# Fetching label rows of an embedding table one by one from SyncE in place of gathers on GpSimd

## The chip, the cores and the metric

The kernel runs on one core of a Trainium2 chip. A core has five engines that run their own instruction streams [...]: TensorE (matmuls, the transposes here too), VectorE (DVE), ScalarE (ACT), GpSimd (POOL) and SyncE (SP), which computes nothing and issues transfers. The metric is the device time of the whole program in microseconds, the median of the timed runs. A profile is a separate execution, recorded by the hardware profiler.

## The reference

The computation is the forward pass of a recommendation model on 16,384 samples. Each sample has 69 feature ids and one label id, all of them rows of an embedding table of 100,001 rows x 96 floats.

```python
u = emb[batch_user]                          # 16384 x 69 x 96
ql = emb[batch_label[:, 0]]                  # 16384 x 96
q = broadcast(ql[:, None, :], u.shape)
z = concatenate([q, u, q - u, q * u], -1)    # 384 wide
h = dice(z @ W1 + b1, a1)                    # 64 wide
att = (h @ W2 + b2) @ W3 + b3                # one number per feature
pre = where(batch_user < 100000, u * att, 0)
pooled = einsum('gf,bfe->bge', window, pre)  # 69 features into 10 groups
x = concatenate([pooled, ql], -1)            # 11 x 96 wide
h = dice(bn(x @ Wf1 + bf1), af1)             # 200 wide
h = dice(bn(h @ Wf2 + bf2), af2)             # 80 wide
return h @ Wf3 + bf3
```

dice(x, a) is (a (1 - p) + p) x with p = sigmoid(x). All values are float32. What matters here: 16,384 x 69 = 1,130,496 feature rows and 16,384 label rows of 384 bytes each are fetched by index from the table in HBM.

## The kernel before, in words

The samples are cut into 32 blocks of 512. The 512 x 69 feature rows of a block are cut into 69 chunks of 512 rows: 64 main chunks (8 samples x 64 features) and 5 tail chunks (512 samples x one feature). Two chunks make a pair, the unit of the main loop: 1,104 pairs in all, 34.5 to a block.

Gathers. `gather` (L226-232) is one indirect transfer issued by GpSimd: it fetches 128 table rows, whose numbers stand in a column of an SBUF tile, one to each of 128 partitions. A pair needs eight of them (`fetch`, L307). TensorE transposes what came (L308), VectorE multiplies it by the label's embedding (L311 or L318), ScalarE copies it (L319).

Label rows. A block's 512 label rows are fetched by four more gathers into a tile `q` (`head_gather`, L238-243), 128 rows each. `head_turn` (L245-249) transposes them on TensorE and puts the result into one of two tiles `qTs`; `head_row` (L251-269) multiplies that by the part of W1 that depends on the label alone. Tile `q` has two buffers.

Indices. `load_ids` (L100-103) has SyncE load one block's indices: 276 columns of feature ids and four of label ids. `map_ids` (L105-109) on VectorE moves the id 100,000 to a row of zeros. Its result, `rows`, is what the feature gathers read.

The rest of a pair's work. `seed` (L275-296) puts the label's share of the hidden layer into PSUM, `hidden` (L322-331) adds the two matmul terms of each chunk (L326) and applies dice (L328-330), `attend_rows` and `spread` (L333-365) turn four pairs of hidden values into attention weights, `pool` (L367-393) contracts them with the gathered rows (L376). When a block is through, its top network runs in ten steps (`top_steps`, L438-449); the last one, `top3`, stores 512 results by a transfer from SyncE (L432).

The order of work is written out by hand. Inside the manual schedule (L470) instructions go to their engines' queues in program order. In step i of the loop (L474-507) stand the seed of pair i-1, the pooling of pair i-8, the attention of pairs i-3 and i-4, the hidden layer of pair i-2 and the fetch of pair i, and after them what a plan (L452-468) has for that step. For block n with first pair `first`, the plan has the load of indices 24 steps ahead, `map_ids` 21, `head_gather` 14, `head_turn` 11 and `head_row` 9 steps ahead. The top network of a block begins 12 steps after its last pair, so the store of its result comes 21 steps after it. The gathered tiles `u` have 14 buffers, and a pair's tile is held until it is pooled 8 steps later.

The semaphores that count a transfer's completion are given out by the framework, which reuses a set of them in turn.

Of the kernel before, what the change touches and what calls it, by code (L numbers as in the profile page):

```python
# [30 lines left out]
F32 = mybir.dt.float32  # L31
# [6 lines left out]
P = 128  # L38
B, F, E, G = 16384, 69, 96, 10
ITEM_NUM = 100000  # L40
# [4 lines left out]
BLK = 512  # L45
NBLK = B // BLK
# [5 lines left out]
NQ = BLK // P  # L52
NT = NCH * 4
NCOL = NT + NQ
NPAIR = NBLK * NCH // 2
S_DICE = float(1.0 / np.sqrt(1.0 + 1e-9))
S_BN = float(1.0 / np.sqrt(1.0 + 1e-5))
# [6 lines left out]
def rec_kernel(  # L64
    ctx: ExitStack,
    tc: tile.TileContext,
    idx: bass.AP,
    emb: bass.AP,
    W1: bass.AP,
    b1: bass.AP,  # L70
# [17 lines left out]
    nc = tc.nc  # L88
# [8 lines left out]
    bpool = ctx.enter_context(tc.tile_pool(name="bpool", bufs=2))  # L97
    xpool = ctx.enter_context(tc.tile_pool(name="xpool", bufs=1))

    def load_ids(n):  # L100
        ids = ipool.tile([P, NCOL], I32, tag="ids", name=f"ids{n}")
        nc.sync.dma_start(out=ids, in_=idx[n : n + 1].rearrange("o p n -> (o p) n"))
        return ids

    def map_ids(n, ids):  # L105

        rows = ipool.tile([P, NT], I32, tag="rows", name=f"rows{n}")
        nc.vector.scalar_tensor_tensor(rows, ids[:, 0:NT], float(ITEM_NUM), ids[:, 0:NT], ALU.is_ge, ALU.add)
        return rows

    ids, rows = {0: load_ids(0)}, {}
# [9 lines left out]
    for i in range(2):  # L121
        nc.vector.tensor_add(Cq[0:E, i, :], w1[:, 0, :], w1[:, 2, :])
    nc.sync.dma_start(
        out=Cq[E : E + 1], in_=b1.rearrange("(o q h) -> o q h", o=1, q=1).to_broadcast([1, 2, H1])
# [101 lines left out]
    def gather(dst, index):  # L226
        nc.gpsimd.indirect_dma_start(  # L227
            out=dst,
            out_offset=None,
            in_=emb,  # L230
            in_offset=bass.IndirectOffsetOnAxis(ap=index, axis=0),
        )

    def chunk(c):

        return divmod(c, NCH)

    def head_gather(n):  # L238

        q = bpool.tile([P, NQ, E], F32, tag="q", name=f"q{n}")  # L240
        for k in range(NQ):
            gather(q[:, k, :], ids[n][:, NT + k : NT + k + 1])
        return q

    def head_turn(n, q):  # L245
        pq = ps_x.tile([E, BLK], F32, tag="x", name=f"pq{n}")
        for k in range(NQ):
            nc.tensor.transpose(pq[:, k * P : (k + 1) * P], q[:, k, :], ident)
        nc.vector.tensor_copy(qTs[n % 2][0:E, 0:BLK], pq)

    def head_row(n):  # L251

        cT = bpool.tile([P, BLK], F32, tag="cT", name=f"cT{n}")
        pc = ps_x.tile([P, BLK], F32, tag="x", name=f"pc{n}")
        for i in range(2):
            nc.tensor.matmul(
                pc[i * H1 : (i + 1) * H1, :],
                Cq[:, i, :],
                qTs[n % 2][:, i * NS : i * NS + BLK],
                start=True,  # L260
                stop=True,
            )
        nc.scalar.copy(cT, pc)

        cU = bpool.tile([P, BLK], F32, tag="cU", name=f"cU{n}")
        pc = ps_x.tile([P, BLK], F32, tag="x", name=f"pc2_{n}")
        nc.tensor.matmul(pc, Cq.rearrange("e i h -> e (i h)"), qTs[n % 2][:, 0:BLK], start=True, stop=True)
        nc.scalar.copy(cU, pc)
        return cT, cU
# [5 lines left out]
    def seed(i):  # L275

        ph = ps_h.tile([P, 512], F32, tag="h", name=f"ph{i}")
        nc.tensor.matmul(ph, zrow[:, 0:P], zrow, start=True, stop=False)  # L278
        (n0, k0), (n1, k1) = chunk(2 * i), chunk(2 * i + 1)
        if n0 == n1 and k1 < NMAIN:  # L280
            nc.scalar.copy(  # L281
                ph.rearrange("h (s f) -> h s f", f=FM), by_field(cs[n0][0][:, k0 * NS : (k0 + 1) * NS])
            )
        elif n0 == n1 and k0 >= NMAIN:
            nc.scalar.copy(ph, cs[n0][1])
        else:
            for j, (n, k) in enumerate([(n0, k0), (n1, k1)]):
                lo, hi = j * H1, (j + 1) * H1
                if k < NMAIN:
                    nc.scalar.copy(  # L290
                        ph[lo:hi].rearrange("h (s f) -> h s f", f=FM),
                        by_field(cs[n][1][lo:hi, k * NS : (k + 1) * NS]),
                    )
                else:
                    nc.scalar.copy(ph[lo:hi], cs[n][1][lo:hi, :])
        return ph
# [36 lines left out]
    def attend_rows(b, ys):  # L333

        pr = ps_x.tile([P, 512], F32, tag="x", name=f"prow{b}")
        for k, y in enumerate(ys):
            nc.tensor.matmul(pr[32 * k : 32 * (k + 1), :], v2, y, start=True, stop=True)  # L337
        row = rpool.tile([P, 512], F32, tag="row", name=f"row{b}")
        nc.scalar.copy(row, pr)  # L339
        return row  # L340

    def attend_tail(i, j, y, uT):

        n, k = chunk(2 * i + j)
        pa = ps_x.tile([E, 512], F32, tag="x", name=f"pa{i}_{j}")
        nc.tensor.matmul(pa, vrep[j * H1 : (j + 1) * H1, :], y[j * H1 : (j + 1) * H1, :], start=True, stop=True)  # L346
        nc.vector.scalar_tensor_tensor(pres[n][:, k - NMAIN, :], pa, bb[0:E], uT[:, j, :], ALU.add, ALU.mult)  # L347
# [88 lines left out]
    cs, pooled, pres, x1s, x2s, qs, us, hs, phs, ys, bands, rws, p1s = ({} for _ in range(13))  # L436

    def top_steps(n):  # L438


        def half(h, part):
            if h == 0 and part == 0:
                x1s[n] = xpool.tile([DH, 2, BLK], F32, tag="x1", name=f"x1_{n}")
            p1s[n] = top1(n, h, part, p1s.get(n))

        steps = [lambda h=h, part=part: half(h, part) for h in range(2) for part in range(4)]
        steps.append(lambda: x2s.__setitem__(n, top2(n)))
        steps.append(lambda: top3(n, x2s.pop(n)))
        return steps
# [4 lines left out]
    def at(step, work):  # L454
        plan.setdefault(step, []).append(work)

    for n in range(NBLK):
        first, end = n * NCH // 2, ((n + 1) * NCH - 1) // 2
        if n > 0:
            at(first - 24, lambda n=n: ids.__setitem__(n, load_ids(n)))  # L460
            at(first - 21, lambda n=n: rows.__setitem__(n, map_ids(n, ids[n])))
            at(first - 14, lambda n=n: qs.__setitem__(n, head_gather(n)))
            at(first - 11, lambda n=n: head_turn(n, qs.pop(n)))
            at(first - 9, lambda n=n: cs.__setitem__(n, head_row(n)))
        for s, work in enumerate(top_steps(n)):
            at(end + POOL_LAG + 4 + s, work)
    for f in range(NTAIL):
        at(2 + 2 * f, lambda f=f: tail_weights(f))

    with tc.manual_schedule():  # L470
        qs[0] = head_gather(0)
        head_turn(0, qs.pop(0))
        cs[0] = head_row(0)
        for i in range(NPAIR + POOL_LAG + 16):  # L474
            if 0 <= i - 1 < NPAIR:
                phs[i - 1] = seed(i - 1)
            if 0 <= i - POOL_LAG < NPAIR:
                k = i - POOL_LAG
                pool(k, us.pop(k), rws[k // 4])
                if k % 4 == 3:  # L480
                    rws.pop(k // 4)
            if 0 <= i - 3 < NPAIR and (i - 3) % 4 == 3:
                b = (i - 3) // 4
                bands[b] = attend_rows(b, [ys[4 * b + k] for k in range(4)])
            if 0 <= i - 3 < NPAIR:
                k = i - 3
                uT = hs.pop(k)[0]
                for j in range(2):
                    if chunk(2 * k + j)[1] >= NMAIN:
                        attend_tail(k, j, ys[k], uT)  # L490
            if 0 <= i - 4 < NPAIR and (i - 4) % 4 == 3:
                b = (i - 4) // 4
                rws[b] = spread(b, bands.pop(b))
                for k in range(4):
                    ys.pop(4 * b + k)
            if 0 <= i - 2 < NPAIR:
                ys[i - 2] = hidden(i - 2, phs.pop(i - 2), *hs[i - 2])
            if i < NPAIR:
                for j in range(2):
                    n, k = chunk(2 * i + j)  # L500
                    if n not in pooled:
                        pooled[n] = bpool.tile([E, G, BLK], F32, tag="pooled", name=f"pooled{n}")
                        pres[n] = xpool.tile([E, NTAIL, BLK], F32, tag="pre", name=f"pre{n}")
                u, uT, quT = fetch(i)
                us[i], hs[i] = u, (uT, quT)
            for work in plan.pop(i, []):
                work()
# [48 lines left out]
```

## Time and profile before

The time is 11,344.07 us, the median of 3 runs (11,340.12 to 11,345.51).

| | profiled execution |
|---|---|
| span | 13,499.4 us |
| granted TensorE clock, mean | 0.658 |
| TensorE busy | 10,109.4 us, 75% |
| GpSimd busy | 8,525.6 us, 63% |
| ScalarE busy | 3,740.6 us, 28% |
| VectorE busy | 3,172.4 us, 24% |
| gathers of feature rows | 8,832, mean 951 ns |
| gathers of label rows | 128, mean 963 ns |
| share of the 16 DMA engines taken by gathers | 15.5% |
| transfers issued by SyncE in the loop | 2 per block |

How to read it: the profile lists an instruction of each engine with its start, its duration, and the idle time ahead of it, and names what ended that idle time. "issue" means that nothing was seen to be waited for. "remote" is a releaser that the profile could not name among this core's instructions. "SPq" and "POOLq" are the instruction streams of SyncE and GpSimd where they issue transfers or wait; this is not counted as busy. [...] Note that the profiled execution is 19% longer than the timed ones.

### The profile page before, as it was taken

The page shows a single profiled execution, that of the slowest core. Times are in us where ns is not written, and L with a number is a line of the kernel's source. Part 1 is how long each engine was busy: PE and PEld are TensorE (multiplying, and loading weights), DVE is VectorE, ACT ScalarE, POOL GpSimd, SP SyncE. Part 2 cuts the span into 40 slices and gives each one's busy share as a digit, 9 for nine tenths or more (in the row PEclk, how much of TensorE's full clock was granted, in tenths as well). Part 3 has the DMA queues.
Part 4 walks back from the last instruction along what each step waited for, and adds up shares of the span by engine and source line. Part 5 has one row for each costly group of instructions (what it writes and reads, how often), then busy time and mean ns, then how long its engine had stood idle before and what let it go on. Part 6 is the DMA issues. An engine that isn't in the chain of part 4 may idle for free.

```text
span 13499.4 us, 108113 instructions
## 1 busy us (share of the span) xinstructions
PE 10109.4 (75%) x41348; PEld 5068.4 (38%) x41348; DVE 3172.4 (24%) x5424; ACT 3740.6 (28%) x6086; POOL 8525.6 (63%) x8966
## 2 busy tenths in 40 slices
PE   4777777778777776777777777777778777787778
PEld 2333333334333333333333333333333333343334
DVE  2222222222222222222222222222222222222222
ACT  1222222223222222222222222222222222232222
POOL 6666666666666666666666666666666666666664
PEclk5666666666666677666666666766666666666657
DMA  1111111111111111111111111111111111111111
GB/s 37 34 34 35 33 34 33 34 35 34 34 34 34 34 34 33 33 34 34 33 34 34 34 34 35 34 33 33 33 35 34 34 33 34 35 34 33 34 32 22
DMA packets 295008, 453.59 MB, mean 34 GB/s; under 512 B 145952, under 2 KB 151104, under 8 KB 294496
## 3 DMA queue, kind: packets, MB, share of 16 engines
q0 software_dynamic: 286720, 440.98, 15.5%
q8 instruction: 331, 5.42, 0.2%
q1 hardware_dynamic: 6142, 4.77, 0.1%
q14 instruction: 181, 1.48, 0.0%
q10 hardware_dynamic: 1634, 0.94, 0.0%
HBM read 446.04 MB, written 0.07 MB: 33 GB/s over the span
## 4 chain that ended last, share of the span: by engine, by line
PE 62%; another core or an unknown queue 15%; issue 12%; ACT 5%; DVE 5%; POOL 1%; DMA 0%; DVEq 0%; POOLq 0%; ACTq 0%
PE ph L326 22%; PE acc L376 15%; PE ptr L308 9%; PE p L406 5%; PE prow L337 4%; PE ph L278 4%; DVE y L330 3%; ACT y L329 2%; PE patt L353 2%; ACT y L328 1%; PE pa L346 1%; DVE quT L311 1%; ACT uT L319 1%; POOL u L227 1%
## 5 line engine op out<-in xcount | busy, mean ns | idle before, releaser
L227 POOL DMA_INDIRECT u<-in_emb,rows x8832 | 8401.6, 951 | 4802.4 <-issue 2351.7
L376 PEld LDWEIGHTS acc<-rw,u 128*96 128x96 f32 x16384 | 2185.5, 230 | 2828.8 <-issue 2828.2
L278 PE MATMUL ph<-zrow 1*128 1x512 bf16 x1104 | 532.2, 482 | 2654.8 <-DVE y L330 1760.5
L319 ACT COPY uT<-ptr 96x512 f32<-96x512 f32 x2208 | 1285.2, 582 | 3713.4 <-DVE quT L311 2616.7
L376 PE MATMUL acc<-rw,u 128*96 128x20 f32 x16384 | 2298.9, 292 | 1.8 <-DVE rw L359 1.3
L308 PEld LDWEIGHTS ptr<-ident,u 128*96 128x96 f32 x8832 | 1312.6, 167 | 1912.8 <-issue 1547.8
L308 PE MATMUL ptr<-ident,u 128*96 128x128 f32 x8832 | 1785.7, 362 | 326.1 <-issue 247.9
L326 PE MATMUL ph<-uT,A 96*64 96x512 f32 x4416 | 1954.0, 955 | 27.4 <-issue 26.7
L326 PE MATMUL ph<-quT,w 96*64 96x512 f32 x4416 | 1915.7, 909 | 54.5 <-issue 53.2
L328 ACT ACTIVATE y<-ph 128x512 f32<-128x512 f32 x1104 | 659.4, 597 | 4602.9 <-remote 2107.1
L330 DVE TENSOR_TENSOR y<-ph,y 128x512 f32<-128x512 f32 x1104 | 763.7, 692 | 4689.6 <-ACT y L329 2396.5
L311 DVE TENSOR_TENSOR quT<-ptr,qT 96x512 f32<-96x512 f32 x2048 | 1340.0, 680 | 1866.9 <-remote 887.1
L385 DVE COPY pooled<-acc 96x160 f32<-96x160 f32 x1008 | 430.6, 427 | 2811.6 <-remote 1020.7
L326 PEld LDWEIGHTS ph<-quT,w 96*64 96x64 f32 x4416 | 491.4, 202 | 1279.1 <-issue 1277.6
L329 ACT ACTIVATE y<-y,a1c,na1c 128x512 f32<-128x512 f32 x1104 | 897.4, 813 | 37.2
L281 ACT COPY ph<-cT 128x512 f32<-128x512 f32 x1008 | 591.4, 587 | 281.5 <-remote 75.0
L406 PE MATMUL p<-pooled,wf 96*100 96x512 f32 x1280 | 620.0, 625 | 6.3 <-issue 4.8
L337 PE MATMUL prow<-y,v 128*32 128x512 f32 x2208 | 546.6, 932 | 79.7 <-issue 41.3
L326 PEld LDWEIGHTS ph<-uT,A 96*64 96x64 f32 x4416 | 307.0, 183 | 766.4 <-issue 696.0
L339 ACT COPY row<-prow 128x512 f32<-128x512 f32 x276 | 161.4, 585 | 864.0 <-remote 345.4
L353 PE MATMUL patt<-ident,row 128*128 128x128 f32 x1104 | 267.9, 386 | 113.4 <-DVE pre L347 88.1
L406 PEld LDWEIGHTS p<-pooled,wf 96*100 96x100 f32 x1280 | 219.7, 181 | 270.1 <-issue 267.3
(71 smaller groups left out, 2535.6 us busy)
## 6 DMA issues: line engine op xcount, KB each, us to landing
u<-in_emb,rows POOLq DMA_INDIRECT x8832
ids<-in_idx SPq DMA_DIRECT2D x32, 140.0 KB
q<-in_emb,ids POOLq DMA_INDIRECT x128
wf<-in_Wf ACTq DMA_DIRECT2D x1, 825.0 KB
out<-res SPq DMA_DIRECT2D x32, 2.0 KB
w<-in_W SPq DMA_DIRECT2D x1, 96.0 KB
wf<-in_Wf ACTq DMA_DIRECT2D x1, 62.5 KB
a1c<-in_a SPq DMA_DIRECT2D x2, 0.2 KB
```

The costliest lines, as they stand in the source:

```text
L227: nc.gpsimd.indirect_dma_start(out=dst, out_offset=None, in_=emb, in_offset=bass.IndirectOffsetOnAxis(ap=index, axis=0),)
L278: nc.tensor.matmul(ph, zrow[:, 0:P], zrow, start=True, stop=False)
L308: nc.tensor.transpose(ptr[:, t * P : (t + 1) * P], u[:, 4 * j + t, :], ident)
L311: nc.vector.tensor_tensor(quT[:, j, :].rearrange("e (s f) -> e s f", f=FM), ptr.rearrange("e (s f) -> e s f", f=FM), by_field(q[:, k * NS ...
L319: nc.scalar.copy(uT[:, j, :], ptr)
L326: nc.tensor.matmul(ph[j * H1 : (j + 1) * H1, :], w, x[:, j, :], start=False, stop=last)
L328: nc.scalar.activation(y, ph, AF.Sigmoid, scale=S_DICE)
L329: nc.scalar.activation(y, y, AF.Identity, bias=a1c, scale=na1c)
L330: nc.vector.tensor_mul(y, ph, y)
L337: nc.tensor.matmul(pr[32 * k : 32 * (k + 1), :], v2, y, start=True, stop=True)
L376: nc.tensor.matmul(pa[:, j, 2 * t : 2 * t + 2, :].rearrange("e n g -> e (n g)"), u[:, 4 * j + t, :], rw[:, i % 4, j, t, :], start=True, st ...
L406: nc.tensor.matmul(p1, w[:, h * DH : (h + 1) * DH], x, start=(k == 0), stop=(k == KTOP - 1))
```

## The change

Blocks 1 to 31 no longer gather their label rows on GpSimd. Instead SyncE loads 32 labels at a time into its registers from a new input `lab` (the labels in plain order), and issues one transfer per label, from the table row that the register names to one partition of `q`. A block takes 16 such parts; part k stands in the plan 31 - k steps ahead of the block, from 31 to 16 steps. Block 0 keeps its four gathers (`first_head`). Tile `q`, what reads it, and everything else stay as they were. The purpose is to take work from GpSimd and give it to SyncE.

```diff
+NLD = 32
...
+    lab: bass.AP,
...
-    def head_gather(n):
-
-        q = bpool.tile([P, NQ, E], F32, tag="q", name=f"q{n}")
+    def first_head():
+
+        q = bpool.tile([P, NQ, E], F32, tag="q", name="q0")
         for k in range(NQ):
-            gather(q[:, k, :], ids[n][:, NT + k : NT + k + 1])
+            gather(q[:, k, :], ids[0][:, NT + k : NT + k + 1])
         return q
+
+    def head_gather(n, part):
+
+        if part == 0:
+            qs[n] = bpool.tile([P, NQ, E], F32, tag="q", name=f"q{n}")
+        k, p = divmod(part * NLD, P)
+        _, at = nc.values_load_multi_w_load_instructions(
+            lab[n : n + 1, part * NLD : (part + 1) * NLD],
+            engines=[mybir.EngineType.SP],
+            min_val=0,
+            max_val=ITEM_NUM,
+            skip_runtime_bounds_check_because="labels are rows of the table",
+        )
+        for i, row in enumerate(at):
+            nc.sync.dma_start(out=qs[n][p + i : p + i + 1, k, :], in_=emb[bass.ds(row, 1), :])
...
-            at(first - 14, lambda n=n: qs.__setitem__(n, head_gather(n)))
+            for part in range(BLK // NLD):
+                at(first - 31 + part, lambda n=n, part=part: head_gather(n, part))
             at(first - 11, lambda n=n: head_turn(n, qs.pop(n)))
...
-        qs[0] = head_gather(0)
-        head_turn(0, qs.pop(0))
+        head_turn(0, first_head())
...
+        "lab": x["batch_label"].reshape(NBLK, BLK),
```

More of the change, by code (lines that the diff above doesn't have):

```diff
@@ L518 @@
     tail = user[:, :, FM:].reshape(NBLK, NQ, P, NTAIL).transpose(0, 2, 3, 1).reshape(NBLK, P, NTAIL * NQ)
-    labels = x["batch_label"].reshape(NBLK, NQ, P).transpose(0, 2, 1)
     window = x["window"]
@@ L523 @@
         wtile[n, :, n, :] = window[:, :FM].T
+    labels = x["batch_label"].reshape(NBLK, NQ, P).transpose(0, 2, 1)
     arrays = {
         "idx": np.concatenate([main, tail, labels], axis=2),
+        "lab": x["batch_label"].reshape(NBLK, BLK),
         "emb": np.concatenate([x["emb"], np.zeros((1, E), np.float32)], axis=0),
```

## The prediction

> **What bounds the kernel now.** I read in turn the page (busy times, clock by slices, the chain that ended last, the costliest groups), the waits of GpSimd, and its instructions in order of time.
>
> ```profile
> PE 10109.4 (75%) x41348; PEld 5068.4 (38%) x41348; DVE 3172.4 (24%) x5424; ACT 3740.6 (28%) x6086; POOL 8525.6 (63%) x8966
> ...
> PEclk5666666666666677666666666766666666666657
> ...
> PE 62%; another core or an unknown queue 15%; issue 12%; ACT 5%; DVE 5%; POOL 1%; DMA 0%; DVEq 0%; POOLq 0%; ACTq 0%
> ```
>
> Read alone, this says TensorE: busiest, at about 0.66 of its clock, and 62% of the chain that ended last. But this execution took 13,499 us and the timed ones 11,344, 16% less. What bounds the timed runs has to fit into 11,344 us.
>
> ```profile
> L227 POOL DMA_INDIRECT u<-in_emb,rows x8832 | 8401.6, 951 | 4802.4 <-issue 2351.7
> ```
>
> ```profile
> POOL u L227 <- issue: 2351.7, 7703, 0.6
> POOL u L227 <- PE acc L376: 860.1, 160, 39.9
> POOL u L227 <- remote: 755.3, 239, 6.0
> ```
>
> ```profile
> 320.13 0.94 POOL L227 DMA_INDIRECT u<-in_emb,rows  x1 [0.30 <-issue]
> 321.38 0.95 POOL L227 DMA_INDIRECT u<-in_emb,rows  x1 [0.31 <-issue]
> 322.63 0.95 POOL L227 DMA_INDIRECT u<-in_emb,rows  x1 [0.30 <-issue]
> ```
>
> The last columns of the middle view are total us, times and longest. 7,703 gathers have only "issue" ahead of them: 2351.7/7703 = 0.305 us, not a wait for anyone but the gap that GpSimd leaves anyway. So a gather is worth 0.947 + 0.304 = 1.25 us, and the starts (320.13, 321.38, 322.63) show exactly that step. The kernel has 8,832 + 128 = 8,960 gathers: 8,960 x 1.2505 = 11,204 us. The trace adds 3.3 us before the first gather and 13,499.4 - 13,369.4 = 130 us after the last. The sum is 11,337 us, beside 11,344 measured. GpSimd in an unbroken row of gathers explains the timed runs to within 7 us; the waits for TensorE (860.1, and most of the "remote") stretch only the profiled execution. I therefore take the timed kernel to be bound by gather issue, with TensorE just fast enough. The last is an inference: no stretch of the trace shows it.
>
> [...]
>
> **The change part by part.**
>
> *Removed:* 31 x 4 = 124 gathers, L242. At 1.2505 us each: 155.1 us of GpSimd. In the timed runs they lie on the path. If nothing else binds, 11,344 - 155 = 11,189 us.
>
> *Added:* 31 x 512 = 15,872 row transfers and 31 x 16 = 496 register loads of 32 labels, all on SyncE. SyncE is in order, so the question is what one row costs there. The nearest rows are the result store and the index load:
>
> ```profile
> L432 SPq DMA_DIRECT2D out<-res x32: 228/258/267, 764.0 to 13497.2; - x32
> ```
>
> ```profile
> L102 SPq DMA_DIRECT2D ids<-in_idx x32: 3/341/701, 0.7 to 12445.5; - x32
> ```
>
> Min/median/max in ns. The store of one 2 KB row is the best model of a 384-byte row: 0.258 us to issue. [...] The trace has a duration, so I take 0.26. Between two copies without a separate wait SyncE leaves about 0.05 us (index load ends at 1.15, next load starts at 1.21). The register load does not occur before. [...] Turning a label into a byte address: unseen; [...] 17 ns, which is also the median of SyncE's semaphore instructions beside the store. I take four to five, 0.08 us; ends 0.02 and 0.15. [...]
>
> A transfer also waits for the earlier one that used its completion semaphore; there are eight in turn. The last store is issued at 13,497.2 and everything has ended at 13,499.4, so a small transfer lands within 2.2 us: 2.2/8 = 0.28 us per row, under the issue time and hidden by it.
>
> *The budget:* a block lasts 11,189/32 = 350 us, or 350/512 = 0.68 us per row. At 0.59 SyncE needs 302 us per block, 86% full: hidden behind the gathers, but not by much.
>
> *What moves, and who waits.* Queued on SyncE behind the rows are the index load (L102) and the result store (L432). SyncE now waits for the store of each block:
>
> ```profile
> SPq L432 <- DVE res L431: 8908.4, 21, 749.2
> ```
>
> Block n's rows follow, in program order, the store of block n-3, done about 49 pairs before block n begins. They must be in place for the transposes 11 pairs before it. That leaves 38 pairs of 10 us, 380 us, for 302 us of work. The index load stands after 7 of the 16 parts, 132 us, so at 36 pairs ahead, and its user (L108, DVE) comes at 21. The first block keeps its gathers, since SyncE could not be early there. All of this costs nothing at 0.59. The four transposes of L248 now wait for several semaphores in place of one each: [...] on a TensorE that waits for gathers anyway; nothing. Row traffic is 15,872 x 384 B = 6.1 MB beside 441 MB; a 2 KB store occupies one engine for some 0.1 us at most, so even if all rows go to one engine that is 1,587 us of it over the run, 14%, on top of 15.5%: gathers land a little later, and nothing waits on their landing (waits of gathers for gathers total 134.8 us, longest 0.3, no more than the usual gap).
>
> Forecast: 11,344 - 155 = 11,189 us, so 1.4% faster.
>
> **The rivals.**
>
> *SyncE becomes the bound (slower).* Then the end is set by 15,872 rows, plus some 15 us before the first, plus what remains once the last block's labels are there: (11 + 34.5) pairs x 10 us + 130 = 585 us. T = 600 + 15,872 r. It passes 11,344 at r = 0.677. At r = 0.75 it gives 12,504 us and at 0.83, 13,774. For it: the margin is 14%, two terms of the sum are unseen, and a register-addressed copy may take longer to issue than the fixed store. Against: the shown part is only 0.31 us, and the remaining 0.36 would have to be all register work.
>
> *TensorE holds the pace (same or less gain).* Removing gathers gives it 5 us less per block. For it: in no 300 us slice of the trace does it reach the timed pace; the best has 1,028 matmuls against 41,348/11,344 x 300 = 1,093 needed. Against: its mean clock in those slices wanders between 0.58 and 0.73, and the timed runs differ by only 5 us, which suits a fixed issue interval better than a wandering clock. Time: between 11,189 and 11,344; 11,266 in the middle, 11,344 if TensorE is at its limit already.
>
> *The label gathers were hidden.* If GpSimd had slack, nothing moves: 11,344 us. The count of 11,337 leaves it none, so I put this with the rival above.
>
> **How the numbers follow.** Forecast 0.74; SyncE bound 0.18; TensorE holding all or part 0.08, of which 0.05 stays within 0.2% of before. So faster 0.77, same 0.05, slower 0.18. The predicted time is the likeliest case, 11,189. The range begins 39 us under it, for a shorter start or tail, and reaches over the TensorE cases to 11,380; together 0.82. SyncE at its limit lies mostly above and is left out.
>
> **What would show it.** Right: 8,836 gathers still 1.25 us apart; label rows on SyncE about 0.6 us apart, with a pause in each block before the store; no wait of L248 for label rows. Wrong: SyncE without a pause, rows 0.7 us apart or more, TensorE at L248 or DVE at L108 waiting for its transfers. If rows are quick and the time still stands, TensorE was the limit. The profiled execution itself, being slowed by TensorE, may hardly change; the timed runs count.

## The result, and the profile after

The changed kernel takes 11,181.65 us, the median of 4 runs (11,178.86 to 11,183.8), beside 11,344.01 us for the kernel before (4 runs, 11,340.12 to 11,345.51). The ratio is 0.9857, with a 95% interval of 0.984 to 0.9874: 162 us less, somewhere between 143 and 182. The prediction was 11,189 us.

The profiled execution of the changed kernel took 11,177 us, as long as the timed ones, so its trace can be read directly. That of the kernel before cannot: it is 19% longer than its timed runs. Differences between the two traces are therefore mostly not effects of the change.

The page of the changed kernel, in turn the busy times, the granted clock by slices, the chain that ended last, and the feature gathers (which now stand at L229):

```profile
PE 9700.5 (87%) x41348; PEld 4721.0 (42%) x41348; DVE 3187.3 (29%) x5424; ACT 3760.0 (34%) x6086; POOL 8404.8 (75%) x8842
...
PEclk6767677677776767767777667776677776677767
...
PE 33%; POOL 32%; issue 16%; DMA 10%; SPq 5%; ACT 2%; DVE 1%; POOLq 0%; ACTq 0%
...
L229 POOL DMA_INDIRECT u<-in_emb,rows x8832 | 8400.1, 951 | 2692.9 <-issue 2459.0
```

TensorE still has the most busy time, 87%, and still the largest share of the chain, though only just. Neither makes it the bound. The waits of GpSimd (total us, times, longest) settle it; these are the three largest rows:

```profile
POOL u L229 <- issue: 2459.0, 8065, 0.3
POOL u L229 <- PE ptr L325: 105.8, 347, 0.3
POOL u L229 <- DMA u<-in_emb,rows: 101.9, 334, 0.3
```

The longest entry of each row is 0.3 us. That is the gap GpSimd leaves between any two gathers, whoever is named as the releaser. Only one entry of the whole view is longer, 2.0 us at the start of the run, for the first indices. GpSimd never stood still for TensorE. Its instructions in order of time show the same step as before:

```profile
320.01 0.95 POOL L229 DMA_INDIRECT u<-in_emb,rows  x1 [0.30 <-issue]
321.26 0.94 POOL L229 DMA_INDIRECT u<-in_emb,rows  x1 [0.30 <-issue]
322.51 0.94 POOL L229 DMA_INDIRECT u<-in_emb,rows  x1 [0.30 <-issue]
```

Counted over the whole trace, 8,836 gathers start between 3.36 and 11,100.37 us: a mean step of 1.2560 us (median 1.249), and 77 us from the last start to the end.

The waits of TensorE show who waits for whom now:

```profile
PE ptr L325 <- DMA u<-in_emb,rows: 1172.1, 1424, 2.7
PE ph L295 <- DVE y L347: 191.7, 303, 1.3
PE pq L265 <- DMA q<-in_emb: 50.3, 24, 46.4
```

TensorE waited 1,424 times for a gather, 1,172 us in all, and its weight loads another 1,527 us: it had room. The last row is the transposes of the label rows, which wait for the new transfers 24 times. Of its 50.3 us one wait takes 46.4. It belongs to block 1. Other blocks' rows have 38 pairs of time; those of block 1 start with the kernel, at 16.8 us, about 23 pairs ahead of their use (34.5 - 11). That is 230 us for some 284 us of rows.

SyncE has the new work. First its waits, then its instructions over a little more than one block (start, us, and the number of like instructions run together):

```profile
SPq L449 <- DVE res L448: 2230.6, 31, 350.3
```

```profile
5000.16 24.75 SPq L260 DMA_DIRECT2D q<-in_emb  x49
5077.57 0.24 SPq L449 DMA_DIRECT2D out<-res  x1
5082.98 121.33 SPq L260 DMA_DIRECT2D q<-in_emb  x224
5204.35 0.38 SPq L104 DMA_DIRECT2D ids<-in_idx  x1
5209.58 156.53 SPq L260 DMA_DIRECT2D q<-in_emb  x288
```

A block's work on SyncE runs from the store at 5,077.57 to 5,209.58 + 156.53 = 5,366.11: 289 us. A block lasts 11,100/32 = 347 us, which leaves 58. SyncE pauses for the result in every block but the first: 31 pauses, 2,230.6 us in all. The last two, 549 us, are long because no label rows are left to fetch; the other 29 take 58 us on average.

The cost of one row comes from the instructions of two lines, min/median/max in ns. L260 is one transfer, L252 the load of 32 labels into registers:

```profile
L260 SPq FUSED_REGOPS  x15872: 37/37/51, 16.8 to 10570.9; - x199
L260 SPq MOVE q<-in_emb x15872: 29/29/38, 16.9 to 10571.0; - x199
L260 SPq DMA_DIRECT2D q<-in_emb x15872: 219/220/343, 16.9 to 10571.1; - x199
```

```profile
L252 SPq TENSOR_LOAD <-in_lab_ptr x496: 1012/1105/1421, 12.1 to 10553.4; - x166
L252 SPq ALU_OP  x496: 42/50/59, 13.2 to 10554.6; - x166
L252 SPq TENSOR_LOAD <-in_lab x496: 3327/3429/3888, 13.3 to 10554.6; - x166
```

A row is three instructions, 0.29 us, and in the median the rows start 0.403 us apart. A load is three instructions too, 1.105 + 0.050 + 3.429 = 4.6 us, or 0.143 us for each of its 32 rows. From start to start, with the loads in it and the steps across a store left out, a row took 0.554 us on average.

### The profile page after: what moved, and what is told of

It is laid out like the page before. It is cut to its first block, busy times and chain, and to the rows that moved or that the text cites. A ratio compares the mean times of both kernels' runs of the same rounds, so it can differ in the third digit from the quotient of the medians.

```text
span 11177.1 us, 157529 instructions
## 1 busy us (share of the span) xinstructions
PE 9700.5 (87%) x41348; PEld 4721.0 (42%) x41348; DVE 3187.3 (29%) x5424; ACT 3760.0 (34%) x6086; POOL 8404.8 (75%) x8842
## 4 chain that ended last, share of the span: by engine, by line
PE 33%; POOL 32%; issue 16%; DMA 10%; SPq 5%; ACT 2%; DVE 1%; POOLq 0%; ACTq 0%
POOL u L229 32%; PE ph L343 12%; DMA u<-in_emb,rows 10%; PE acc L393 9%; PE p L423 4%; SPq L260 3%; PE ptr L325 3%; PE prow L354 2%; SPq L252 2%; PE ph L295 2%; PE pa L363 1%; ACT y L346 1%; DVE y L347 1%; ACT y L345 1%; PE patt L370 1%
## 5 line engine op out<-in xcount | busy, mean ns | idle before, releaser
L229 POOL DMA_INDIRECT u<-in_emb,rows x8832 | 8400.1, 951 | 2692.9 <-issue 2459.0
L325 PE MATMUL ptr<-ident,u 128*96 128x128 f32 x8832 | 2006.4, 353 | 1189.5 <-DMA u<-in_emb,rows 1172.1
L325 PEld LDWEIGHTS ptr<-ident,u 128*96 128x96 f32 x8832 | 1221.0, 155 | 3053.7 <-DMA u<-in_emb,rows 1526.9
L393 PEld LDWEIGHTS acc<-rw,u 128*96 128x96 f32 x16384 | 2048.5, 217 | 531.8 <-issue 531.2
L393 PE MATMUL acc<-rw,u 128*96 128x20 f32 x16384 | 2160.4, 282 | 1.8 <-DVE rw L376 1.3
L343 PE MATMUL ph<-uT,A 96*64 96x512 f32 x4416 | 1793.5, 904 | 0.0
L343 PE MATMUL ph<-quT,w 96*64 96x512 f32 x4416 | 1671.9, 847 | 0.0
L343 PEld LDWEIGHTS ph<-quT,w 96*64 96x64 f32 x4416 | 442.8, 194 | 1074.9 <-issue 1074.9
L423 PE MATMUL p<-pooled,wf 96*100 96x512 f32 x1280 | 659.4, 660 | 1.2 <-DVE x L427 0.8
L354 PE MATMUL prow<-y,v 128*32 128x512 f32 x2208 | 455.2, 909 | 0.0
L423 PE MATMUL p<-pre,V 96*100 96x512 f32 x640 | 314.6, 625 | 0.0
```

Source lines behind the costliest of these rows:

```text
L229: nc.gpsimd.indirect_dma_start(out=dst, out_offset=None, in_=emb, in_offset=bass.IndirectOffsetOnAxis(ap=index, axis=0),)
L325: nc.tensor.transpose(ptr[:, t * P : (t + 1) * P], u[:, 4 * j + t, :], ident)
L343: nc.tensor.matmul(ph[j * H1 : (j + 1) * H1, :], w, x[:, j, :], start=False, stop=last)
L393: nc.tensor.matmul(pa[:, j, 2 * t : 2 * t + 2, :].rearrange("e n g -> e (n g)"), u[:, 4 * j + t, :], rw[:, i % 4, j, t, :], start=True, st ...
L423: nc.tensor.matmul(p1, w[:, h * DH : (h + 1) * DH], x, start=(k == 0), stop=(k == KTOP - 1))
```

## The experiments

The theory: GpSimd is in an unbroken row of gathers, so the end moves by the gathers removed, and SyncE's rows lie in its shade. Rival 1: SyncE's in-order queue is the bound, or close enough to cost something. Rival 2: TensorE holds the pace, and removed gathers are worth less than their issue time.

One thing has to be known ahead. On the four chips that the experiments ran on, the kernel before takes 13,414 to 13,530 us, close to its first profile, and not 11,344. (On which chip the runs at 11,344 and 11,182 us were made is not recorded, so that the chip is the reason is not shown.) No experiment ran at the pace of 11,344. What this does to the comparison became a question of its own, and the last two groups of runs are about it. Expectations that stand on 11,344 were written before this was seen.

### The kernel before again, and the label rows left out

`e1_before_again` is the kernel before, unchanged.

> The kernel before, unchanged, for a second profile of it. Theory (gather issue sets the pace, the slow first profile was that execution's own): 11,344 us, and if this profile runs at that pace, GpSimd shows no wait longer than its usual gap of 0.3 us. Rival (TensorE sets the pace of the kernel before): GpSimd waits for TensorE here too, some hundred us in all or more.

It took 13,430.77 us. GpSimd is not unbroken here (waits of GpSimd):

```profile
POOL u L227 <- issue: 2358.9, 7724, 1.8
POOL u L227 <- PE acc L376: 855.9, 159, 42.4
POOL u L227 <- remote: 673.6, 227, 5.7
POOL u L227 <- PE ptr L308: 551.8, 245, 4.6
```

Unlike the rows of the changed kernel above, three of these have longest entries of 4.6 to 42.4 us: real waits, two of them for TensorE by name. That is the sign that the expectation gave for rival 2, but at 13,430 us it says nothing of a kernel that takes 11,344. And TensorE itself is stretched without a visible cause. Two places of the same trace, with the same kind of weight load in the top network:

```profile
9002.52 0.25 PEld L406 LDWEIGHTS p<-pooled,wf 96*100 96x100 f32 x2 [1.24 <-issue]
9003.91 0.16 PEld L406 LDWEIGHTS p<-pooled,wf 96*100 96x100 f32 x1 [1.15 <-issue]
9005.31 0.25 PEld L406 LDWEIGHTS p<-pooled,wf 96*100 96x100 f32 x2 [1.24 <-issue]
...
9025.02 0.17 PEld L406 LDWEIGHTS p<-pooled,wf 96*100 96x100 f32 x1 [0.26 <-issue]
```

At 9,025 us they stand 0.43 us apart (0.17 + 0.26), at 9,002 us groups of them stand 1.4 us apart, with nothing named that they wait for. So single instructions are held up in bursts. In the trace of the changed kernel shown above, the same weight loads never have more than 0.57 us of idle time ahead of them, but for one at the end of the run.

`e3_no_label_rows` is the changed kernel with neither gathers nor transfers for the label rows of blocks 1 to 31: they use block 0's label rows.

```diff
...
-            for part in range(BLK // NLD):
-                at(first - 31 + part, lambda n=n, part=part: head_gather(n, part))
-            at(first - 11, lambda n=n: head_turn(n, qs.pop(n)))
+            at(first - 11, lambda n=n: head_turn(n, qs[0]))
...
```

> Leaves out the label rows of blocks 1 to 31 altogether: every block uses those of block 0; nothing for SyncE to fetch. Theory (15,872 transfers on SyncE are wholly hidden): as the changed kernel, 11,182 us, within 0.2%. Rival (the transfers cost something through late rows, shared DMA engines or waits): faster than the changed kernel by over 22 us.

Measured: 13,250.26 us, ratio to before 0.9857 (0.9839 to 0.9875), that is 192 us less by the ratio. Removing the 124 gathers and adding nothing helps even where GpSimd has waits. 124 gathers at 1.256 us would be 156 us, which the interval (168 to 216 us) leaves out. At the step that gathers have here, waits and all, they fit: 1.490 us on average in this run's trace, and 124 x 1.490 is 185. That a removed gather is worth its step with the waits in it is not shown; only the sum agrees. What the run was made for, whether the transfers on SyncE cost anything, is answered by `e7_after_again` below, the changed kernel at this pace: it takes 2,254 us more than this run, so here the rival of the expectation came true.

### Half the rows, and the whole change again

`e2_half_rows` and `e8_half_rows_again` keep two of a block's four label gathers and fetch the other 256 rows on SyncE.

```diff
...
+        if part < BLK // NLD // 2:
+            return
...
+            at(first - 14, lambda n=n: half_gather(n))
...
```

> Half the change: per block two label gathers stay on GpSimd, 256 rows go to SyncE. Theory (each gather issue is worth 1.256 us of the end, nothing else counts): 62 gathers fewer than before, 11,344 - 78 = 11,266 us. Rival (the gain is a stall that the bunch of four gathers caused, or TensorE is at its limit after the first few): 11,182 or 11,344, not the middle.

> Half the change again (two label gathers per block stay on GpSimd, 256 rows go to SyncE). If before is at 11,344 here: theory (each gather issue 1.256 us of the end) 11,266 us; rival (the gain is the bunch of four, or stops early) 11,182 or 11,344. If before is near 13,430: slower than it, 13,811 us, as in the run before; then the order of work around TensorE counts and not the gathers.

Measured: 13,811.14 us, ratio 1.0283 (1.0259 to 1.0307), and 13,804.93 us, 1.0272 (1.0245 to 1.0298). Half the change makes the kernel slower here, although SyncE stands still ahead of each of the 32 stores: 5,377 us of idle time in the first run. So a pause of SyncE is not enough, at this pace, for its rows to be free. The expectation of the second run adds that the order of work around TensorE would then be what counts; the run does not show that.

`e7_after_again` is the changed kernel without an edit.

> The changed kernel, unchanged, beside the kernel before on the same chip. In the runs before this the kernel before took 13,433 us on its chip, not 11,344. Theory A (where the kernel before is at gather pace, the change is worth 155 to 162 us): a chip with before at 11,344 gives 11,182. Theory B (the pace of TensorE differs from chip to chip and then hides the gathers): a chip with before near 13,430 gives 13,250 to 13,450 here, within 1.5% of before. Rival C (the changed kernel escapes whatever holds the kernel before): 11,182 on a chip where before takes 13,430.

Measured: 15,504.35 us, ratio 1.1547 (1.1528 to 1.1567), which none of the three theories of the expectation had. The change that gains 1.4% where the kernel before takes 11,344 us loses 15% where it takes 13,430. SyncE in order of time shows why:

```profile
5289.11 237.24 SPq L260 DMA_DIRECT2D q<-in_emb  x224
5526.39 0.45 SPq L104 DMA_DIRECT2D ids<-in_idx  x1
5532.07 240.24 SPq L260 DMA_DIRECT2D q<-in_emb  x288
5772.41 0.24 SPq L449 DMA_DIRECT2D out<-res  x1
```

The 224 rows that took 121.33 us take 237.24, and the store, next in SyncE's queue, comes 0.1 us after the last row: no pause. The pauses for the result fell from 31 to 2 (waits of SyncE), both after the last row, and TensorE now waits for label rows at its transposes:

```profile
SPq L449 <- DVE res L448: 585.7, 2, 389.5
```

```profile
PE pq L265 <- DMA q<-in_emb: 971.9, 18, 77.4
```

That is rival 1 of the prediction, sign by sign: SyncE without a pause, rows over 0.7 us apart on average, TensorE at the transposes (L265 here) waiting. Its formula, T = 600 + 15,872 r, solved for the profiled execution gives r = (15,437 - 600)/15,872 = 0.935 us. The trace has 0.934.

### Gathers taken away, rows added

`e6_seven_gathers` is the changed kernel with 1,104 feature gathers left out: the eighth part of each pair is read from the seventh.

```diff
...
-                gather(u[:, 4 * j + t, :], rows[n][:, 4 * k + t : 4 * k + t + 1])
-                nc.tensor.transpose(ptr[:, t * P : (t + 1) * P], u[:, 4 * j + t, :], ident)
+                if 4 * j + t < 7:
+                    gather(u[:, 4 * j + t, :], rows[n][:, 4 * k + t : 4 * k + t + 1])
+                nc.tensor.transpose(ptr[:, t * P : (t + 1) * P], u[:, min(4 * j + t, 6), :], ident)
...
```

> The changed kernel with one of the eight feature gathers of each pair left out (1,104 gathers fewer; that eighth tile is read from the seventh), TensorE's, VectorE's and ScalarE's work unchanged. Theory (gather issue alone, TensorE has room): 11,182 - 1,104 x 1.256 = 9,795 us. Rival (TensorE is right behind): it stops falling on the way, anywhere from 10,000 to 11,182 us, and GpSimd shows long waits for TensorE.

Measured: 14,140.83 us, ratio 1.0527 (1.0505 to 1.0548). It has only 2 pauses of SyncE for the result, 538.4 us, both after its last row: SyncE was the bound, so this run could not price a gather where GpSimd is the bound. As a test of the theory it is inconclusive.

`e9_rows_576` and `e10_rows_640` add 64 and 128 rows per block, fetched into a spare tile that nothing reads.

```diff
...
+                if part < MORE:
+                    at(first - 31 + part, lambda n=n, part=part: more_rows(n, part))
...
```

> The changed kernel with 64 rows more per block on SyncE, into a spare tile that nobody reads. At 0.562 us per row, as its trace shows, SyncE needs 324 us per block of the 349 there are. Theory (hidden as long as it is under a block's time): 11,182 us, up to 25 us more for the first block, whose rows come later. Rival (SyncE's rows already cost): slower by over 0.3%.

> 128 rows more per block, into a spare tile: 640 x 0.562 = 360 us per block, over the 349 there are. Theory (SyncE becomes the bound as soon as its rows exceed a block): 13 + 31 x 360 + 45.5 pairs x 10.1 + 76 = 11,710 us, and SyncE no longer waits for the result. Rival (rows are late but something else absorbs it): stays at 11,182 us.

Measured: 16,593.56 us, ratio 1.2362 (1.2342 to 1.2383), and 17,637.22 us, 1.3129 (1.3106 to 1.3153). Each step of 31 x 64 = 1,984 rows costs (16,594 - 15,504)/1,984 = 0.549 us a row, then (17,637 - 16,594)/1,984 = 0.526. Once SyncE has no pause, an added row is paid in full at the end, and its price is near the 0.554 us of a row that is not held up. The hold-up itself did not grow with the rows. With the steps across a store left out, as for the 0.554, a row took 0.926 us in `e7_after_again` and 0.851 in `e10_rows_640`. That is 0.372 x 15,872 = 5,904 us of hold-up in the one and 0.297 x 19,840 = 5,892 us in the other.

### What is held up: the instruction or the transfer

`e14_fixed_rows` writes the table addresses into the program, so that a row is one SyncE instruction in place of three and no registers are loaded. It fetches as many rows of the same size, but others than the labels name.

```diff
...
-        for i, row in enumerate(at):
-            nc.sync.dma_start(out=qs[n][p + i : p + i + 1, k, :], in_=emb[bass.ds(row, 1), :])
+        for i in range(NLD):
+            r = (n * BLK + part * NLD + i) * 6 % ITEM_NUM
+            nc.sync.dma_start(out=qs[n][p + i : p + i + 1, k, :], in_=emb[r : r + 1, :])
```

> The row transfers of the changed kernel with table addresses written into the program: one SyncE instruction per row in place of three, and no registers loaded. It fetches other rows of the table than the labels name, the same number of the same size. Where the kernel before takes about 13,430 us: theory A, that each instruction of SyncE is held up there, has the excess of a row over its undisturbed time fall from 0.38 us to about a third of it, so that SyncE gets pauses for the result again and the time lies between 13,300 and 14,300 us; theory B, that each transfer is held up, keeps the excess of 0.38 us per row, and with 0.26 us of issue a row then takes about 0.64 us, which also frees SyncE (15,872 x 0.64 = 10,158 us), so the two are told apart by the row's pitch in the trace, 0.35 to 0.45 us by A and 0.60 to 0.70 us by B, and not by the time. Where the kernel before takes 11,344 us: 11,182 us as the changed kernel, since SyncE's work is hidden there anyway.

Measured: 13,721.24 us beside 13,413.79, ratio 1.0225 (1.0207 to 1.0244). A row takes 0.431 us on average and 0.295 in the median. With the median taken as its undisturbed time, the excess is 0.136 us, a good third of the 0.372 of three instructions a row. Theory A held, on pitch and on time: the excess goes with SyncE's instructions, not with the transfers. A fixed price per instruction it is not, since the rows added above brought no more of it. Waits for an earlier transfer have a part too: the profile names 251 of them, 151 us of the some 2,160 us of excess, and with semaphore changes missing from the trace it may not name all. SyncE pauses again in this run (waits of SyncE):

```profile
SPq L443 <- DVE res L442: 3921.3, 18, 419.1
```

The view counts only pauses whose semaphore change was recorded; by the idle time ahead of the stores, SyncE pauses for all 32, 6,859 us in all. Yet the kernel is slower than the kernel before, and by the ratios (1.0225 and 0.9857) some 490 us slower than `e3_no_label_rows`, which fetches nothing. So on these chips 15,872 instructions on an engine with time to spare still cost something at the end. By the waits that the profile names, it reaches the gathers through TensorE: those of GpSimd for the pooling matmuls (L376 of the kernel before) are 1,500.8 us here and 1,485.2 in `e2_half_rows`, beside 947.9 in `e3_no_label_rows` and 855.9 in `e1_before_again`. Why TensorE is later was not found.

### GpSimd slowed, so that it is the bound again

To ask the theory's question on these chips, GpSimd has to be the bound there. Three kernels have two selects on a small tile after every gather. They change nothing that is used and make a gather's step about 2.04 us; the 2.35 of the expectation was a guess.

```diff
...
+        for _ in range(2):
+            nc.gpsimd.affine_select(
+                out=slow,
+                in_=slow,
...
```

`e11_slow_before` is the kernel before with it, `e12_slow_after` the changed kernel with it. `e13_slow_both` is the added part alone: the gathers stay and are used, and SyncE fetches the 512 rows as well, into a spare tile.

> The kernel before with two small GpSimd instructions after every gather (affine_select on a 128 x 256 scratch tile that nobody reads), so that a gather with what follows takes about 2.35 us in place of 1.25 and GpSimd is the bound whatever TensorE and SyncE do. Expected about 8,960 x 2.35 + 80 = 21,140 us; the pitch is to be read from its trace and is what the next two are reckoned with.

> The changed kernel with the same two instructions after every gather. Theory (with GpSimd the bound, each gather that is taken away is worth its pitch, and 15,872 row transfers on SyncE lie beside it): e11_slow_before less 124 pitches, about 290 us at 2.35 us, a ratio of 0.986. Rival (SyncE's rows or what they do to the others hold the end): no gain, or slower, as in e7_after_again.

> The added part alone, in the same slowed form: all label gathers stay on GpSimd and are used, and SyncE fetches the 512 rows of each block as well, into a spare tile that nobody reads. Theory: the added part is hidden, as e11_slow_before within 0.2%. Rival (the added part costs by itself): slower by over 0.5%.

| | median us | ratio to the kernel before (13,530 us) |
|---|---|---|
| `e11_slow_before` | 18,328.37 | 1.3551 (1.3515 to 1.3586) |
| `e12_slow_after` | 18,086.21 | 1.3372 (1.3337 to 1.3407) |
| `e13_slow_both` | 18,332.18 | 1.3553 (1.3518 to 1.3589) |

GpSimd hardly waits in these: at most 1.8 us at a time, in the first. From the waits of GpSimd and of TensorE in `e11_slow_before`:

```profile
POOL u L229 <- issue: 1601.1, 8676, 1.4
```

```profile
PE ptr L320 <- DMA u<-in_emb,rows: 6311.1, 4151, 3.4
```

The change as a whole gives 18,328 - 18,086 = 242 us; 124 gathers at the step of 2.038 us in the trace of `e12_slow_after` are 253, and the runs of one kernel differ by up to 53. The added part alone gives +4 us (18,332 - 18,328), less than the runs of one kernel differ: it is hidden. SyncE in `e12_slow_after` waits for the result in every block, and its rows are 0.554 us again:

```profile
SPq L461 <- DVE res L460: 9123.3, 32, 570.6
```

Here the theory's two halves are shown apart: with GpSimd the bound, removed gathers are paid out at their step, and added rows cost nothing while SyncE has a pause.

## Why the prediction was right

**GpSimd as the bound.** Right, and for the changed kernel now seen in a trace of the timed pace. For the kernel before it is still only counted. The count, 8,960 x 1.2505 + 3.3 + 130 = 11,337, had two errors that cancel, so that it came within 7 us was in part luck. The step is 1.2560 us, since the mean gather takes 0.951 us and not the median of 0.947 that was used. And the 130 us after the last gather came from a held-up execution; the changed kernel has 77, and `e11_slow_before` 76. With these the count is 8,959 x 1.2560 + 80 = 11,333, 11 us short.

**124 gathers removed.** Predicted 155.1 us, measured 162, from 11,344 to 11,182; 124 x 1.256 is 156. The 6 us left are inside the interval of the ratio (143 to 182). `e12_slow_after` against `e11_slow_before` repeats the step with another price: 253 by the step of its trace, 242 measured.

**The row on SyncE.** Predicted 0.59 us, measured 0.554, but the terms were off both ways. Issue: 0.26 from the store of before, measured 0.22. Registers: the kernel before loads none, and what the 0.59 holds for them was the author's estimate, as was the 0.83 of the rival; no trace showed either. For the registers it was too high; this trace has 0.143, pointer and all. Arithmetic: 0.08 taken, four to five times the 17 ns of a semaphore instruction. In `e14_fixed_rows` a row without it has a median step of 0.295, with it 0.403, so it was 0.11. Copy and gap together: 0.26 + 0.05 = 0.31 predicted, 0.295 in that run. The errors in part cancel, so the sum is better than its terms.

**The budget.** 302 us of 350 predicted; 289 of 347 measured, with pauses of 58 us in place of 48. The completion semaphores, eight in turn with 1,984 of the rows on each in the trace, cost nothing that the waits of SyncE show: its rows at L260 have two waits, 0.3 us at most. The rows' packets, one of 384 bytes each, occupied the DMA engines for 517 us in all, where 1,587 had been allowed. No block was late except block 1, for which the prediction's 38 pairs do not hold: it looked at the first block, which has its gathers, and not at the second. The 46.4 us of TensorE at L265 reach no wait of GpSimd, so they cost nothing.

**TensorE.** "Just fast enough" understated it for the changed kernel: TensorE waits 1,172 us for gathers. The rival that it holds the pace was drawn from a trace in which it was held up, and fell. One statement was wrong: that the profiled execution may hardly change. It took 11,177 us.

**SyncE as the bound.** Given 0.18, and false where the kernel before takes 11,344 us. But the prediction's margin of 14% counts only where SyncE's instructions run freely. In the experiments that leave GpSimd as it is they do not, and the rival came true with its formula right to 0.001 us per row. That the profile of before ran at this slower pace was known; that SyncE's own rows would be slower in such an execution was not thought of.

**What stays open.** At 11,344 us the theory rests on the count, the one comparison and the trace of the changed kernel; the runs that separate its two halves had a slowed GpSimd, at the other pace. And it is open why instructions are held up in the experiments and not in the runs at 11,344 and 11,182 us. The granted clock of TensorE does not settle it: it was lower in `e12_slow_after` (0.600), where SyncE's rows are fast, than in `e7_after_again` (0.652), where they are not. One trait goes with the hold-ups: records per us in the trace (instructions, packets and semaphore changes) are 60.7 in the changed kernel's profile, and between 32.6 and 38.1 in every trace of the experiments and in the first profile of before. Semaphore changes are missing in most of the latter: 66,562 in `e7_after_again` beside 198,250, of the same 157,529 instructions. In the slowed kernels, which need little more than that per us, most of them are there (172,577 in `e12_slow_after`) and the rows are fast. A limit on recording that holds the engines back would fit these figures. That is the author's guess and was not shown: no experiment sets recording apart from the chip, and the timed runs there are as long as the profiled ones.

## What to carry to other kernels

When a profile is longer than the timed runs, find the engine whose count times step gives the timed span: eight thousand gathers at one step named the bound that busy times and the chain of the page both missed. Rows on SyncE were free here where GpSimd was the bound and SyncE paused in every block (`e13_slow_both`: +4 us, with 32 pauses, 9,370.8 us in all). Where it had no pause, added rows were paid in full (`e9_rows_576` and `e10_rows_640`: 0.549 and 0.526 us a row). So price one unit of such work and state the pause. A pause alone is no proof: in `e2_half_rows` and `e14_fixed_rows` SyncE paused in every block, GpSimd waited for TensorE (1,485.2 and 1,500.8 us at the pooling matmuls), and the kernels were still 2 to 3% slower than the kernel before. A margin of 14% on 15,872 rows of three small instructions each was not enough where such instructions are held up: there (`e7_after_again`) the same change cost 15%.

## What the runs showed of the hardware

- In the trace of the changed kernel a SyncE transfer of one 384-byte row with its address from a register started every 0.403 us in the median, with two register instructions, 37 and 29 ns, ahead of each. In `e14_fixed_rows`, with a fixed address, one started every 0.295 us.
- In the trace of the changed kernel a load of 32 values into SyncE's registers took 4.6 us: 1.105 for the pointer, 3.429 for the values, which is 0.107 us for each of the 32.
- In the same trace an indirect gather of 128 rows of 384 bytes kept GpSimd busy for 0.951 us in the mean and was followed by a gap of 0.30 us: 8,836 of them ran at a mean step of 1.256 us.
- In `e1_before_again` groups of TensorE's weight loads stand 1.4 us apart (9,002.52, 9,003.91 and 9,005.31 us) with no wait that the profile names, while the ten gathers from 9,012.62 to 9,023.85 us start 1.25 us apart. In `e7_after_again` the transfer of a row took SyncE up to 1,410 ns, beside 343 at most in the changed kernel's first trace. The excess per row was 0.372 us with three instructions to a row (`e7_after_again`) and 0.136 with one (`e14_fixed_rows`), and the rows added in `e10_rows_640` brought none (5,892 us in all beside 5,904).
